# The order of the second batch's query tiles in two causal attention layers, and the store of the last rows

## The chip, the cores and the metric

The kernel is one program on 1 core of a Trainium2 chip. The metric is device time in microseconds (us) of one execution; three runs of the kernel before took 1541.68, 1546.62 and 1547.99, median 1546.62. The core's engines are TensorE (PE), VectorE (DVE), ScalarE (ACT), GpSimd (POOL) and SyncE (SP, which here issues DMAs); each works through its own instructions in order and waits on semaphores for the others.

## The reference

The input is x, two batches of 2048 tokens with 256 features, float32. Two layers are computed, each as x = x + attention(xn) + ffn(xn) with xn = layernorm(x):

```python
attn = einsum('bqd,bkd->bqk', q, k); attn = where(causal, -inf, attn) / sqrt(256)
attention = einsum('bqk,bkd->bqd', softmax(attn), v)
```

The feed-forward part of layer 0 is two shared experts and a routing of each token to 2 of 8 experts. That of layer 1 picks 255 of 2048 tokens of each batch by a router weight, sends them through a small transformer block, and leaves the other tokens as they are. Attention is causal over the 2048 tokens of a batch, so query tile i (128 rows) needs the keys of tiles 0 to i only: (i + 1) x 128 columns of scores.

## The kernel before, in words

The rows of x stay on chip in eight blocks of 512 rows (`x_blocks`, names x0 to x7; four blocks are a batch). A query tile is 128 rows; a batch has 16 of them, tiles 0 to 15, and tile i belongs to block i // 4 of its batch.

The program runs through: attention of layer 0 (line 348 gives its tile order), the routed experts (`run`, lines 671 on), the shared experts, in whose gaps the token selection of batch 0 is worked, and attention of layer 1, in whose gaps the selection of batch 1 is worked (`side`, `beside`, `step`). Both layers call the same function `attention` with the same list `in_turn`: the 16 tiles of the first batch upwards, and then the 16 tiles of the second batch downwards.

For each tile `attention` does this:

1. `scores` (L251 to L272). For each chunk of up to 512 keys PE makes a 128 x 512 score tile, in banks ps_sc and ps_tr by turns. DVE adds the causal mask on the last 128 columns (`tri`, L260), and copies the chunk into `row` with its maximum (L262). After the last chunk DVE reduces the maxima (L268), and ACT takes the exponential of the whole row at once (L270), up to 128 x 2048.
2. `turn` (L301, L303). POOL splits the float32 row into two planes of 16-bit halves for each chunk, and SP issues a DMA that transposes the planes (`across`).
3. `join` (L281, L282). DVE and ACT each copy one half of the transposed words back into a float32 tile, pT (six buffers). A join is put into the queues of DVE and ACT five pieces of work (`LAG`) after its chunk was turned, or when the values need it, whichever is earlier.
4. `average` (L316, L326). PE multiplies pT with the values, one product for each 128 keys, in bank ps_pv, and DVE scales the result and adds it to the row block.

Step 4 of a tile is issued behind step 1 of a later tile. The rule is in these lines, in which `p[2]` is the list of a waiting tile's chunks:

```python
for tile, later in zip(tiles, tiles[1:] + [None]):
    pending.append(turn(*scores(*tile)))
    if later:
        meet(later)
    while sum(len(p[2]) for p in pending[:-1]) >= 3:
        average(*pending.pop(0))
```

So a tile is averaged as soon as the waiting tiles other than the newest hold three chunks or more. `meet` projects the queries of a block of four tiles when the first tile of the block comes up (L594 in layer 0, L1387 in layer 1); the projected queries have two buffers.

The order in which the instructions stand in each engine's queue is made at build time by a scheduler, which may put an instruction that is ready early ahead of one that was written earlier.

Beside the attention of layer 0 the token rows are scattered to their experts' places by 64 indirect DMAs on POOL (L580), and the first expert weights (L684, 512 KB each) are loaded by SP ahead of the experts (L705). Beside the attention of layer 1 the selection (L1171, L1183, L1192, L1209 for its heads, L1002, L1263, L1275 for its norm and its feed-forward part, L1252 for its residual) ends with a scatter of the chosen rows (L1284); then `write_back` loads the gains by SP, 256 KB a piece, and DVE adds them to x (L1297). At the end a loop stores the eight blocks in order, 512 KB each (L1407); the scheduler puts each store into SP's queue near where its block becomes final.

Of the kernel before, what the change touches and what calls it, by code (L numbers as in the profile page):

```python
# [17 lines left out]
P = 128  # L18
B, S, D = 2, 2048, 256
NB = 8  # L20
BPB = NB // B
# [25 lines left out]
def transformer_kernel(ctx: ExitStack, tc: tile.TileContext, a: dict, out: bass.AP):  # L47
    nc = tc.nc
# [17 lines left out]
    x_blocks = []  # L66
# [8 lines left out]
    for g in range(NB):  # L75
# [8 lines left out]
        out=tri, in_=tri, compare_op=ALU.is_ge, fill=NEG, base=0, pattern=[[-1, P]], channel_multiplier=1  # L84
# [5 lines left out]
        out=before, in_=before, compare_op=ALU.is_gt, fill=0.0, base=0, pattern=[[1, P]], channel_multiplier=-1  # L90
# [27 lines left out]
    def step():  # L118
        while side:
            traced = nc.cur_bb.bb.instructions  # L120
            n = len(traced)
            got = next(side[0], step)
            for i in nc.cur_bb.bb.instructions[n:]:
                behind(i)
            held[0] = got == HOLD
            if got is not step:
                return
            side.pop(0)
# [216 lines left out]
            average(*late)  # L345


    in_turn = [(0, i) for i in range(S // P)] + [(1, i) for i in reversed(range(S // P))]

# [8 lines left out]
    with ExitStack() as l0:  # L360
# [8 lines left out]
        for dst, name in ((wq, "wq0"), (wk, "wk0")):  # L369
            turned = weight(work, name, "qT")  # L370
            ps = bank("mm")
            for ec in range(2):
                for dc in range(2):
                    k = (2 * ec + dc) * P
# [10 lines left out]
        parts = work.tile([P, 4, D], F32, tag="xn", name="parts", bufs=1)  # L385
# [286 lines left out]
    with ExitStack() as moe:  # L672
# [57 lines left out]
        for t in range(LIKELY):  # L730
            product, activated = run(t)
            if t >= LIKELY // 3:
                for dst, src in (next(coming, (None, None)),):
                    if dst is not None:
                        i = nc.scalar.dma_start(dst, src)
# [17 lines left out]
    for j, v in enumerate(_FREQ):  # L753
# [5 lines left out]
        out=head_of, in_=head_of, compare_op=ALU.is_ge, fill=0.0, base=0, pattern=[[-HD, 8]], channel_multiplier=1  # L759
    )  # L760
    nc.gpsimd.affine_select(
        out=head_of, in_=head_of, compare_op=ALU.is_ge, fill=0.0, base=HD - 1, pattern=[[HD, 8]],
# [640 lines left out]
    attention(att, in_turn, project_q1, values1, before_tile1)  # L1403
    while side:
        step()
    for g in range(NB):
        nc.sync.dma_start(  # L1407
            out[g * 512 : (g + 1) * 512, :].rearrange("(j p) d -> p j d", p=P), x_blocks[g]
        )


_PI = 3.1415925
# [58 lines left out]
```

## Time and profile before

| | |
|---|---|
| median of three runs | 1546.62 us |
| profiled execution | 1543.37 us, of which span 1541.7 us |
| mean granted PE clock | 0.993 |
| PE idle within the span | 63.5 us (1541.7 less 1478.2) |
| layer 0, batch 1: first scores | 213.11 us |
| routed experts: first matmul | 360.08 us |
| layer 1, batch 1: first scores | 1322.20 us |
| last value product ends, last store issued | 1536.92 us, 1537.47 us |

The times of places are counted from the start of the span. A line of PE's timeline gives start, duration, line, the tiles written and read, the shape, the number of records (a float32 matmul leaves two), and in brackets the time that PE was idle just before and what ended it. A line of the waits reads: who waited for whom, us in total, times, longest us. A row of the windows gives, for a stretch, busy time and count of PE, weight loads, DVE, ACT and POOL, then the granted PE clock (1.00 is full), the DMA engines' mean busy share, and GB/s.

### The profile page before, as it was taken

The numbers are of one execution on the slowest core, as the hardware profiler recorded it, in microseconds if no ns is written. First come the engines' busy times: TensorE is split into PE (matmuls) and PEld (weight loads), VectorE is DVE, ScalarE is ACT, GpSimd is POOL, SyncE is SP. The second block draws the span as 40 slices with busy tenths as digits, with TensorE's granted clock in tenths as the row PEclk, the third lists the DMA queues.
The fourth block names the chain that finished last, engine by engine and source line by source line (L and its number), as shares of the span: only waits on it lengthen the run. The fifth ranks groups of instructions, "written<-read, shape, count | busy, mean of one in ns | idle before, by whom it ended". The sixth has DMA issues, their size and how long they took to land.

```text
span 1541.7 us, 17887 instructions
## 1 busy us (share of the span) xinstructions
PE 1478.2 (96%) x5828; PEld 1050.5 (68%) x5828; DVE 697.3 (45%) x2055; ACT 442.0 (29%) x831; POOL 410.2 (27%) x596
## 2 busy tenths in 40 slices
PE   7999899998999999999999999999999998999998
PEld 4566566567888888888565565566675765577665
DVE  6346333343222222222244445866546468666354
ACT  2443233242111111111112212114633532344233
POOL 3554577532111111110122210231003213421132
PEclk9899999999999999999999999999999999999999
DMA  4844556666879888965001110040004425621144
GB/s 152 255 109 120 135 139 138 149 138 150 209 215 226 239 234 256 261 189 158 28 28 41 42 34 21 28 150 18 11 11 92 115 67 106 165 57 23 29 119 102
DMA packets 290558, 183.49 MB, mean 119 GB/s; under 512 B 192960, under 2 KB 265408, under 8 KB 290464
## 3 DMA queue, kind: packets, MB, share of 16 engines
q1 hardware_dynamic: 255168, 134.95, 36.0%
q10 hardware_dynamic: 27664, 26.53, 5.6%
q0 software_dynamic: 7632, 20.86, 4.4%
q8 instruction: 47, 0.77, 0.2%
q14 instruction: 47, 0.39, 0.1%
HBM read 93.14 MB, written 45.14 MB: 90 GB/s over the span
## 4 chain that ended last, share of the span: by engine, by line
PE 28%; issue 10%; DVE 7%; POOL 3%; DMA 2%; ACT 2%; SPq 0%; POOLq 0%; ACTq 0%; DVEq 0%
PE ps_tr L1338 6%; PE ps_sc L1338 6%; PE ps_pv L1357 5%; POOL planes L301 3%; DMA across<-planes 2%; PE ps_mm L1209 1%; PE ps_mm L1171 1%; DVE x L1368 1%; PE ps_sc L251 1%; PE ps_mm L801 1%; PE ps_mm L1192 1%; PE ps_pv L316 1%; PE ps_mm L1275 1%; DVE row L262 1%; ACT pr L1183 1%
## 5 line engine op out<-in xcount | busy, mean ns | idle before, releaser
L301 POOL COPY planes<-row 128x512 uint16<-128x512 uint16 (+3 forms) x320 | 167.7, 569 | 306.8 <-ACT row L270 293.8
L282 ACT COPY pT<-across 128x512 uint16<-128x512 uint16 (+3 forms) x160 | 106.3, 677 | 226.9 <-DMA across<-planes 211.7
L251 PE MATMUL ps_sc<-xnT,qT 128*128 128x512 f32 (+3 forms) x384 | 161.2, 541 | 0.3 <-DVE qT L150 0.2
L714 DVE SCALAR_TENSOR_TENSOR hid<-ps_tr,be,act 128x256 f32<-128x256 f32 x144 | 63.0, 479 | 197.9 <-PE ps_tr L705 192.9
L713 ACT ACTIVATE act<-ps_sc,be 128x256 f32<-128x256 f32 x144 | 60.4, 470 | 302.1 <-PE ps_sc L705 302.1
L1327 POOL DMA_INDIRECT ya<-sorted_y,place x64 | 62.2, 973 | 318.0 <-DVE x L1368 224.9
L316 PE MATMUL ps_pv<-vg,pT 128*128 128x256 f32 x544 | 129.0, 390 | 12.4 <-ACT pT L282 12.0
L705 PE MATMUL ps_sc<-xT,rw 128*128 128x256 f32 x576 | 136.2, 379 | 1.6 <-POOL xT L698 1.6
L705 PE MATMUL ps_tr<-xT,rw 128*128 128x256 f32 x576 | 136.1, 379 | 0.0
L316 PE MATMUL ps_pv<-v,pT 128*128 128x256 f32 x544 | 128.4, 381 | 7.0 <-ACT pT L282 4.6
L720 PE MATMUL ps_pv<-rw,hid 128*128 128x256 f32 x576 | 132.0, 382 | 0.0
L698 POOL COPY xT<-xs 128x512 uint16<-128x512 uint16 x72 | 51.3, 758 | 299.8 <-issue 281.9
L316 PEld LDWEIGHTS ps_pv<-vg,pT 128*128 128x128 f32 x544 | 104.6, 195 | 37.6 <-ACT pT L282 17.5
L1338 PE MATMUL ps_sc<-xnT,sw 128*128 128x512 f32 x256 | 121.9, 594 | 0.1
L1338 PE MATMUL ps_tr<-xnT,sw 128*128 128x512 f32 x256 | 122.0, 593 | 0.0
L316 PEld LDWEIGHTS ps_pv<-v,pT 128*128 128x128 f32 x544 | 101.3, 190 | 29.1 <-ACT pT L282 7.9
L705 PEld LDWEIGHTS ps_sc<-xT,rw 128*128 128x128 f32 x576 | 109.4, 190 | 16.8 <-POOL xT L698 2.0
L705 PEld LDWEIGHTS ps_tr<-xT,rw 128*128 128x128 f32 x576 | 109.5, 190 | 14.8
L720 PEld LDWEIGHTS ps_pv<-rw,hid 128*128 128x128 f32 x576 | 105.0, 190 | 21.2 <-DVE hid L714 6.7
L1357 PE MATMUL ps_pv<-sw,hid 128*128 128x256 f32 x512 | 117.5, 380 | 0.0
L1357 PEld LDWEIGHTS ps_pv<-sw,hid 128*128 128x128 f32 x512 | 96.6, 190 | 18.7 <-issue 6.2
L281 DVE COPY pT<-across 128x512 uint16<-128x512 uint16 (+3 forms) x160 | 68.8, 436 | 89.2 <-DMA across<-planes 88.3
(319 smaller groups left out, 1936.7 us busy)
## 6 DMA issues: line engine op xcount, KB each, us to landing
rw<-in_rw SPq DMA_DIRECT2D x108, 512.0 KB, 4.6
sorted_x<-zero ACTq DMA_DIRECT2D x13, 768.0 KB, 6.6
sorted_y<-y SPq DMA_DIRECT2D x36, 256.0 KB, 4.8
be<-biases SPq DMA_DIRECT2D x36, 132.0 KB, 4.5
table<-xn SPq DMA_DIRECT2D x8, 514.0 KB, 3.7
x<-in_x SPq DMA_DIRECT2D x8, 512.0 KB, 6.8
gains<-zero ACTq DMA_DIRECT2D x8, 512.0 KB, 3.2
gain<-gains SPq DMA_DIRECT2D x16, 256.0 KB, 2.7
```

The source lines that it names most:

```text
L251: product = nc.tensor.matmul(ps[:, :w], lhsT=qT[:, dc, (i % 4) * P : (i % 4 + 1) * P], rhs=xnT[g0 + k][:, dc, :w], start=(dc == 0), stop=( ...
L281: nc.vector.tensor_copy(words[:, :, 1], flat[:, :w]),
L282: nc.scalar.copy(words[:, :, 0], flat[:, w : 2 * w]),
L301: nc.gpsimd.tensor_copy(planes[:, h * w : (h + 1) * w], halves[:, :, 1 - h])
L316: product = nc.tensor.matmul(pv[:, :D], lhsT=turned[k][:, j : j + P], rhs=values[g0 + k][:, j // P, :D], start=(c + j == 0), stop=(c + j = ...
L705: nc.tensor.matmul(ps[:, k * TT : (k + 1) * TT], lhsT=we_in[:, dc, (h + k) * P : (h + k + 1) * P], rhs=xT[:, dc, :], start=(dc == 0), stop ...
L713: activated = nc.scalar.activation(act, p1[:, at], AF.Silu, bias=b1[:, hc])
L714: nc.vector.scalar_tensor_tensor(hid[:, h + k, :], p2[:, at], b2[:, hc], act, op0=ALU.add, op1=ALU.mult)
L720: product = nc.tensor.matmul(po[:, r, :], lhsT=hid[:, hc, r * P : (r + 1) * P], rhs=w3[:, hc, :], start=(hc == 0), stop=(hc == 3),)
L1327: nc.gpsimd.indirect_dma_start(out=ya, out_offset=None, in_=sorted_y, in_offset=bass.IndirectOffsetOnAxis(ap=place[rank][:, t : t + 1], ax ...
L1338: product = nc.tensor.matmul(ps, lhsT=ww[:, dc, hc * P : (hc + 1) * P], rhs=xnT[g][:, dc, :], start=(dc == 0), stop=(dc == 1),)
L1357: product = nc.tensor.matmul(po[:, :D], lhsT=hid[:, hc, j * P : (j + 1) * P], rhs=w["sw3", n][:, hc, :], start=(hc == 0), stop=(hc == 3),)
```

## The change

The first batch's tiles keep their order, in both layers. The second batch's tiles run as 15, 0, 14, 1, 13, 2, 12, 3, and then 4 to 11. At the end the block that holds the last tile is stored last, in two parts: its first three tiles of rows, and the last tile of rows (128 rows, 128 KB) by itself.

```diff
-    in_turn = [(0, i) for i in range(S // P)] + [(1, i) for i in reversed(range(S // P))]
+    in_turn = [(0, i) for i in range(S // P)]
+    in_turn += [(1, i) for k in range(4) for i in (15 - k, k)] + [(1, i) for i in range(4, 12)]
...
-    for g in range(NB):
-        nc.sync.dma_start(
-            out[g * 512 : (g + 1) * 512, :].rearrange("(j p) d -> p j d", p=P), x_blocks[g]
-        )
+    b, i = in_turn[-1]
+    last = b * BPB + i // 4
+    for g in [g for g in range(NB) if g != last] + [last]:
+        parts = (0, 3, 4) if g == last else (0, 4)
+        for lo, hi in zip(parts, parts[1:]):
+            nc.sync.dma_start(
+                out[g * 512 + lo * P : g * 512 + hi * P, :].rearrange("(j p) d -> p j d", p=P),
+                x_blocks[g][:, lo:hi, :],
+            )
```

## The prediction

> **What bounds the kernel now.** I read the engines' busy times first, then the waits of TensorE (PE), then PE's timeline in the two stretches the edit reorders, then one tile's way through all engines. Page part 1:
>
> ```profile
> PE 1478.2 (96%) x5828; PEld 1050.5 (68%) x5828; DVE 697.3 (45%) x2055; ACT 442.0 (29%) x831; POOL 410.2 (27%) x596
> ```
>
> PE is busy for 1478.2 of 1541.7 us, and the edit does not change the set of matmuls. A gain can only come from the 63.5 us in which PE idles, a loss only from new idling. Of the waits of PE the first entry is
>
> ```profile
> PE ps_pv L316 <- ACT pT L282: 16.6, 11, 3.7
> ```
>
> a value product that waits for its transposed probabilities. PE's timeline shows where this happens in the second batch of layer 0 (start, duration, records; in brackets the idle time before and its releaser):
>
> ```profile
> 284.89 5.45 PE L316 MATMUL ps_pv<-vg,pT 128*128 128x256 f32 x24 [1.44 <-ACT pT L282]
> ...
> 295.91 5.02 PE L316 MATMUL ps_pv<-vg,pT 128*128 128x256 f32 x22 [0.42 <-ACT pT L282]
> ...
> 309.75 6.27 PE L316 MATMUL ps_pv<-vg,pT 128*128 128x256 f32 x20 [2.37 <-ACT pT L282]
> ```
> ```profile
> 350.91 2.00 PE L316 MATMUL ps_pv<-vg,pT 128*128 128x256 f32 x8 [0.41 <-DVE x L326]
> 353.75 1.56 PE L316 MATMUL ps_pv<-vg,pT 128*128 128x256 f32 x6 [0.84 <-ACT pT L282]
> 356.68 1.80 PE L316 MATMUL ps_pv<-vg,pT 128*128 128x256 f32 x6 [1.37 <-ACT pT L282]
> 360.08 1.99 PE L705 MATMUL ps_sc<-xT,rw 128*128 128x256 f32 x8 [1.59 <-POOL xT L698]
> ```
>
> Together 8.44 us, of which 4.21 in the drain into the experts. The 20 records at 309.75 also took 6.27 us where 20 x 0.216 = 4.3 is usual (8 take 1.73): 1.95 lost to the clock. So this stretch wastes 10.4 us. In layer 1 the same kind of wait is 2.10 (at 1482.29) and 0.37, 0.77, 1.39 in the drain: 4.63. In all 15 us is what better cover could win; other waits there belong to the token selection beside it.
>
> How long is a tile's way from scores to values? Tile 14 of batch 1 in layer 0:
>
> ```profile
> 232.04 1.45 PE L251 MATMUL ps_tr<-xnT,qT 128*128 128x384 f32 x4
> ...
> 235.80 1.88 ACT L270 ACTIVATE row<-row,nmx 128x1920 f32<-128x1920 f32 x1
> ...
> 238.89 4.28 POOL L301 COPY planes<-row 128x512 uint16<-128x512 uint16 x8
> ...
> 243.51 0.77 ACT L282 COPY pT<-across 128x512 uint16<-128x512 uint16 x1 [5.74 <-DMA across<-planes]
> ```
>
> Scores end at 233.33; the first pT is there at 244.28, 10.95 us later; its four chunks follow 1.4, 1.5 and 0.8 us apart, faster than PE eats them (1.73 per chunk). PE had 12.9 us of other work between (value products 6.9, the next scores 6.0), so nothing waited.
>
> **The change, part by part.** Costs used: a 512-column score chunk 1.72 us (128: 0.43), a value product 0.432 per 128 keys, a query projection 3.44.
>
> *The reorder, layer 0.* No instruction is added but one store. What moves is the cover. `average` runs once the waiting tiles ahead of the newest hold three chunks. In the old order that puts a large tile between a tile's scores and its values. Now the next tile is a one-chunk tile, and with it the large tile's average falls due. The instruction order of the changed program shows what lies on PE between scores 14 and values 14: scores 1 (0.86), values 0 (0.43), scores 13 (6.02, pulled ahead), a quarter projection (0.86): 8.2 us. Against 10.95 that is a stall of 2.8. Bounds: 0.8, if POOL's scatters ahead of the planes (L580, about 2 us of the 10.95) were all done, to 2.8; eight scatters still stand there, so I take 2.8.
>
> Behind it a queue forms. On ACT, exp 13 stands behind tile 14's joins and behind tile 1's, and on DVE the last score pass of 13 stands behind the same joins. Counting from the end of scores 14: joins of 14 done 14.6; planes of 1 follow those of 14 and one scatter, transposed at 15.0, joined 15.5; then mask, pass and maximum on DVE to 16.4, exp 13 to 18.6 (1.8+0.2), scatters 1.1 as seen for tile 14, first planes 1.1, transpose 3.4, join 0.8: 25.0. PE by then has done values 14 (10.95 to 17.4), scores 2, values 1 and half a chunk of 12: 20.4. Stall 4.6 (3.5 without scatters, 4.9 if all three wait). Scores 12 follow values 13, and values 12 have scores 3, three quarters of a projection, values 2 and scores 4 as cover, 7.8 us and 0.2 of waiting for the query copy; exp 12 is on time, so the way is 8.5 to 9.6 (exp 1.68): stall 1.2, with that wait (0.8 to 1.9). Tiles 0 to 7 have covers of 9 us and more against about 8. The three expert weight loads (1.5 MB on SP), which caused the 2.37, now stand ahead of tile 6's transposes, where the cover is 14 us: I take 1.0 (0 to 2.4).
>
> *The drain, both layers.* Tile 11 is last, and between its scores and values stands only values 10: 11 x 0.432 = 4.75. Its way in a quiet kernel follows from tile 3 in layer 1:
>
> ```profile
> 1519.83 1.88 PE L251 MATMUL ps_sc<-xnT,qT 128*128 128x512 f32 x4
> ...
> 1523.39 0.72 ACT L270 ACTIVATE row<-row,nmx 128x512 f32<-128x512 f32 x1 [5.76 <-DVE nmx L268]
> ...
> 1529.43 2.00 PE L316 MATMUL ps_pv<-v,pT 128*128 128x256 f32 x8 [0.37 <-ACT pT L282]
> ```
>
> Scores end at 1521.54, values at 1529.43: 7.9; an exp over 1536 is 1.57 and not 0.72: 8.75. Stall 4.0 in each layer, where the small tiles lost 4.21 and 2.53. Chunks two and three come within 1.73 of each other and add nothing.
>
> *The clock.* Here rule and rows part. The Trainium skill ("TensorE: Matmul & The Clock Gate", Part 1) says that PE falls to half clock after an idle window of some 3.4 us and needs about as long of work to recover: 1.7 us lost for a gap over 3.4, nothing under. The rows of the stretches:
>
> ```profile
> 160.00:180.00 20.00, 15.99 (x49) 11.06 (x50) 6.72 (x21) 5.47 (x7) 8.81 (x14) 0.83 0.55 125
> ...
> 300.00:320.00 20.00, 17.64 (x53) 10.55 (x52) 5.65 (x18) 4.99 (x8) 4.30 (x10) 0.91 0.84 175
> ...
> 1300.00:1320.00 20.00, 16.47 (x80) 9.51 (x79) 16.56 (x37) 5.49 (x7) 9.08 (x15) 1.00 0.77 176
> ```
>
> The column after POOL is the granted clock. After a wait of 3.69 at 162.16, 24 records took 8.11 for 5.2 (2.9 lost); after 2.37, 1.95 lost; after 3.53 at 1305.96, nothing. So the length alone does not decide, and short gaps can cost; mean 1.6. By the rule the gaps 4.6, 4.0 and 4.0 cost 1.7 each, 5.1; by the rows 2.8, 4.6, 4.0, 4.0 cost 1.6 each, 6.4. I take the rows.
>
> Layer 0: 2.8 + 4.6 + 1.2 + 1.0 + 4.0 + 3 x 1.6 = 18.4, less 10.4: **+8.0**.
>
> *Layer 1.* The token selection's matmuls lie between the tiles. Before values 14 PE has 8.2 us, the way without scatters is 9.3 (DVE 1.9, exp 2.1, planes 1.1, transpose 3.4, join 0.8): 1.1. Scores 13 come late here, so its values have 11 us of cover and wait for nothing. Values 12: cover 7.4 and some 0.5 of selection waits, way 9.5 (the joins stand on DVE behind the residual adds L1252): 1.6. The next selection step, L1002, loses the 5.2 us of scores that covered its norm and gets values 12: 0.9. The gain adds L1297, each held by a load, stand on DVE ahead of the passes of tiles 4 to 6 as they did of 10 and 9: 1.5 for 2.10. Drain 4.0 + 1.6. Sum 10.7 less 4.63: +6.1. While PE waits for values the selection chain goes on, so some of its waits (7.4 us from 1338 to 1431) vanish: -1.0 (0 to -3).
>
> *The stores.* Four blocks of 512 KB used to end up late; now block x4 leaves in the middle, x7 and x5 under later tiles, all beside matmuls. SP issues them in order, so x4's store, which waits for tile 3's add, holds back the next gain load and the transposes of tile 5; 13 us of cover there, and 0.6 us an issue, so nothing, up to 1 if that cover fails. At the very end 128 KB lands instead of 512: 3.2 us for 512 and 2.7 for 256 (the gain loads) give about 2.45: -0.75.
>
> Layer 1 with the stores: **+4.3**. Sum +12.3. The profiled execution took 1543.37 (span 1541.7 and 1.7 around it): 1555.7. The median, 1546.62, is 3.25 above that run: I forecast **1558.9** as median.
>
> **The rivals.** *Uncovered large tiles*, as summed: chance 0.5, 1553 to 1565. *It spreads further*: every clock loss is the 2.9 seen once (4 x 1.3 more), the scatters hold tile 13 fully and the weight loads bite as before (+1.7), so +19.2, 1565.8; for it speaks that joins, passes and exps share strict queues; against it, that the small tiles of layer 0 have ample cover: 0.17. *It cancels*: the clock mostly stays up, as after the 3.53, and the selection absorbs layer 1's waits: 12.3 - 6.4 - 2 = +3.9, 1550.5: 0.25. *The small tiles really fill*: the place is values 14, 13 and 12 of both layers. If a large tile's first pT comes within the 8.2 us of cover, these waits and the queue behind exp 13 are gone, and with the weight loads and gain adds hidden too only the two drains of 4.0 stay of the 15.0 us: 8.0 - 15.0 - 0.75 = -7.75, 1538.9. It decides at 8.2, and the trace has 10.95, which only an empty POOL brings near: 0.08. That the drain with small tiles was the larger waste is true only for layer 0 (4.21 for 4.0).
>
> **How the numbers follow.** Something like 0.5% (7.7 us) is what a measurement of this kernel tells from no change. The likeliest case lies over it mostly, the second wholly, the third under it: slower 0.66, within 0.26, faster 0.08. The range reaches over these three and, with the bounds of the unknown terms, some 10 us to either side of the sum; it leaves out the gain and the case of every bound at one end: 1549 to 1570.
>
> **What would show it.** In the changed profile: a bracket of 2 to 3 us before values 14 and of 4 to 5 before values 13 in layer 0 (about 253 and 267 us), 4 us before the last 24 records of both layers, granted clock under 1.00 beside them, "PE ps_pv L316 <- ACT pT L282" up from 16.6 to about 30, and the last store under 4 us before the end. I am wrong if PE runs from scores 14 to values 12 without brackets, if the clock stays 1.00, or if the loss sits in the selection's lines (L1192, L1002).

## The result and the profile after

The changed kernel takes 1552.95 us (median of 18 runs, 1547.87 to 1557.53) and the kernel before, on the same chip, 1545.08 (18 runs, 1541.68 to 1549.73). The ratio is 1.0048, 95% interval 1.0036 to 1.0060, so the change costs about 7.4 us. The forecast was 1558.9 with a range of 1549 to 1570: the sign and the range held, the size (+12.3) was too large.

Some short names are used from here on. "Scores 14" and "values 14" are the score matmuls and the value products of tile 14 of the second batch. Its cover is what PE has to do between the two. Its way is the time from the end of its scores to its first transposed probabilities (pT). PE waits when the way is longer than the cover.

The profiled execution of after is one of its slower ones: 1557.31 us, span 1555.6, mean granted clock 0.987. First its page, part 1, and the two first entries that concern value products in the waits of PE:

```profile
PE 1486.3 (96%) x5828; PEld 1053.9 (68%) x5828; DVE 699.6 (45%) x2055; ACT 441.9 (28%) x831; POOL 410.5 (26%) x596
```
```profile
PE ps_pv L316 <- ACT pT L282: 18.5, 13, 3.5
...
PE ps_pv L316 <- DVE pT L281: 5.4, 2, 3.7
```

The same 5828 matmuls keep PE busy for 8.1 us longer. PE waits only 5.8 us more (69.3 for 63.5). Of the 8.1, 6.4 lie in the two stretches that the edit reorders (4.6 in layer 0, 1.8 in layer 1), and these grew by 10.4 us together. So more than half of the profiled difference is matmuls that ran slower, and a table of waits alone would miss it. PE's timeline of layer 0's second batch shows both (start, duration; in brackets the idle time before):

```profile
259.57 9.53 PE L316 MATMUL ps_pv<-vg,pT 128*128 128x256 f32 x30 [3.71 <-DVE pT L281]
272.74 5.45 PE L316 MATMUL ps_pv<-vg,pT 128*128 128x256 f32 x24 [0.63 <-DVE x L326]
278.34 1.13 PE L316 MATMUL ps_pv<-vg,pT 128*128 128x256 f32 x4 [0.15 <-ACT pT L282]
293.80 6.05 PE L316 MATMUL ps_pv<-vg,pT 128*128 128x256 f32 x26 [1.84 <-ACT pT L282]
...
361.73 8.37 PE L316 MATMUL ps_pv<-vg,pT 128*128 128x256 f32 x24 [3.33 <-ACT pT L282]
371.78 1.99 PE L707 MATMUL ps_sc<-xT,rw 128*128 128x256 f32 x8 [1.68 <-POOL xT L700]
```

These are values 14, values 13 (two rows), values 12, values 11 and the first expert. Thirty records of value products take 6.64 us where nothing disturbs them, and 9.53 behind the wait of 3.71; 24 records take 5.45, and 8.37 behind the wait of 3.33. The granted clock, the column of the windows after POOL's, shows the same places, with a full clock between them:

```profile
260.00:280.00 20.00, 19.22 (x70) 14.72 (x70) 6.96 (x24) 7.63 (x12) 11.94 (x18) 0.87 0.71 141
280.00:300.00 20.00, 18.16 (x64) 11.31 (x63) 9.36 (x32) 8.26 (x14) 14.20 (x20) 1.00 0.55 125
...
360.00:380.00 20.00, 16.59 (x62) 13.62 (x63) 3.60 (x8) 5.25 (x8) 5.29 (x10) 0.83 0.37 67
```

In layer 1 the rows that matter are values 12, the selection's L1004, values behind the gain adds, and the drain on tile 11:

```profile
1453.98 3.70 PE L316 MATMUL ps_pv<-v,pT 128*128 128x256 f32 x16 [1.67 <-DVE pT L281]
1459.24 0.81 PE L1004 MATMUL ps_mm<-ident,hn 128*128 128x128 f32 x4 [1.56 <-DVE hn L1024]
1491.52 2.00 PE L316 MATMUL ps_pv<-v,pT 128*128 128x256 f32 x8 [1.60 <-ACT pT L282]
...
1544.95 7.14 PE L316 MATMUL ps_pv<-v,pT 128*128 128x256 f32 x24 [3.33 <-ACT pT L282]
```

Two stretches sum this up. Layer 0's runs from the first scores of the second batch's tile 15 to the experts' first matmul; layer 1's from its first scores of that tile to the end of the span. Layer 0's was 360.08 - 213.11 = 146.97 us and is 371.78 - 216.30 = 155.48: +8.51. Layer 1's was 219.50 and is 1555.6 - 1334.24 = 221.36: +1.86, the stores included. The spans differ by 13.9. Of this, 3.19 lie ahead of the first changed instruction (213.11 and 216.30); in the nine other kernels below that leave everything ahead of it unchanged, it began at anything from 208.75 to 215.45, so that part is spread between executions. So a profile of one execution is read by stretches here and not by its span.

### The profile page after: what moved, and what is told of

It is laid out like the page before. It is cut to its first block, busy times and chain, and to the rows that moved or that the text cites. A ratio compares the mean times of both kernels' runs of the same rounds, so it can differ in the third digit from the quotient of the medians.

```text
span 1555.6 us, 17898 instructions
## 1 busy us (share of the span) xinstructions
PE 1486.3 (96%) x5828; PEld 1053.9 (68%) x5828; DVE 699.6 (45%) x2055; ACT 441.9 (28%) x831; POOL 410.5 (26%) x596
## 4 chain that ended last, share of the span: by engine, by line
PE 28%; issue 10%; DVE 6%; DMA 3%; POOL 3%; ACT 1%; SPq 0%; POOLq 0%; ACTq 0%; DVEq 0%
PE ps_tr L1340 6%; PE ps_sc L1340 6%; PE ps_pv L1359 5%; POOL planes L301 3%; DMA across<-planes 2%; PE ps_pv L316 2%; PE ps_mm L1173 1%; DVE x L1370 1%; PE ps_mm L1211 1%; PE ps_sc L251 1%; PE ps_mm L1265 1%; PE ps_mm L803 1%; PE ps_mm L1194 1%; PE ps_tr L251 1%; PE ps_mm L1277 1%
## 5 line engine op out<-in xcount | busy, mean ns | idle before, releaser
L282 ACT COPY pT<-across 128x512 uint16<-128x512 uint16 (+3 forms) x160 | 105.7, 677 | 219.3 <-DMA across<-planes 203.8
L316 PE MATMUL ps_pv<-vg,pT 128*128 128x256 f32 x544 | 134.8, 401 | 15.8 <-ACT pT L282 11.5
L316 PE MATMUL ps_pv<-v,pT 128*128 128x256 f32 x544 | 130.9, 385 | 10.6 <-ACT pT L282 7.0
L316 PEld LDWEIGHTS ps_pv<-vg,pT 128*128 128x128 f32 x544 | 107.6, 201 | 43.2 <-ACT pT L282 22.1
L316 PEld LDWEIGHTS ps_pv<-v,pT 128*128 128x128 f32 x544 | 102.1, 192 | 35.3 <-ACT pT L282 14.9
```

What stands on the lines that cost most here:

```text
L282: nc.scalar.copy(words[:, :, 0], flat[:, w : 2 * w]),
L316: product = nc.tensor.matmul(pv[:, :D], lhsT=turned[k][:, j : j + P], rhs=values[g0 + k][:, j // P, :D], start=(c + j == 0), stop=(c + j = ...
```

## The experiments

Every kernel below was timed beside the kernel before on the same chip, in rounds on several chips, so ratios are compared rather than medians (the median of before was 1544.5 to 1545.2). Stretches are of the one profiled execution; without the change they were 146.97 and 219.50. They contain whatever the clock did in that execution.

| kernel | median us | ratio to before, 95% | layer 0 | layer 1 |
|---|---|---|---|---|
| after | 1552.95 | 1.0048 [1.0036, 1.0060] | 155.48 | 221.36 |
| layer0_alone | 1554.65 | 1.0061 [1.0037, 1.0086] | 153.80 | 219.60 |
| layer1_alone | 1545.85 | 1.0008 [0.9996, 1.0019] | 145.32 | 219.30 |
| end_at_11 | 1552.60 | 1.0052 [1.0037, 1.0067] | 153.54 | 222.46 |
| pairs_alone | 1548.28 | 1.0027 [1.0016, 1.0038] | 150.58 | 219.04 |
| longer_cover | 1549.69 | 1.0031 [1.0019, 1.0042] | 153.53 | 215.66 |
| longer_cover_pairs | 1548.67 | 1.0026 [1.0013, 1.0039] | 156.54 | 216.44 |
| filled_end | 1550.17 | 1.0035 [1.0024, 1.0047] | 152.73 | 218.74 |
| store_alone | 1543.99 | 1.0000 [0.9988, 1.0012] | 146.90 | 223.52 |
| no_scatters_before | 1538.88 | 0.9960 [0.9944, 0.9975] | 140.27 | 221.08 |
| no_scatters_after | 1547.67 | 1.0022 [1.0010, 1.0034] | 150.44 | 219.71 |
| no_scatters_covered | 1534.64 | 0.9928 [0.9909, 0.9947] | 142.84 | 217.82 |
| layer1_covered | 1540.09 | 0.9961 [0.9946, 0.9975] | 143.87 | 216.61 |

### One layer at a time

```diff
+    in_turn1 = [(0, i) for i in range(S // P)] + [(1, i) for i in reversed(range(S // P))]
...
-    attention(att, in_turn, project_q1, values1, before_tile1)
+    attention(att, in_turn1, project_q1, values1, before_tile1)
```

(layer0_alone, with the old stores; layer1_alone has the two lists exchanged and the split store.)

> New order in layer 0 only; layer 1's order and the stores are those of before. Before is 1545.1 us, after 1553.0. Theory A (large tiles whose values come due behind a one-chunk tile, tile 11's uncovered drain, and half clock behind both gaps; these are worst in layer 0, where exp carries no selection work but the queues of ACT and DVE do): the profile of after lost 8.5 us in this stretch, some 3 of it clock that varies between runs, so +5 to +8, 1550 to 1553; waits of about 3.7 us before values 14 and 3.3 before values 11. Rival B (the loss is shared evenly by the two layers): +3 to +4, 1548.5. Rival C (the loss is the store or lies in layer 1): 0, 1545.

> New order in layer 1 only, with the split store; layer 0 as before. Theory A: the profile of after lost 1.9 us in this stretch with the store's 1.3 taken off already, so 0 to +2, 1545 to 1547; waits of about 3.3 before values 11 and under 2 before values 14, 13 and 12. Rival B (even shares): +3 to +4 less nothing, 1548.5. Rival C (layer 1 carries the loss): +7, 1552. In its profile scores 15 of the second batch in layer 0 should begin at 213 us as before, not at 216, if the three microseconds ahead of the edit were caused by the edit; if they begin anywhere from 213 to 217, that is a spread of runs.

Layer 0 alone costs 9.4 us (1.0061, 5.7 to 13.3 by the interval), a little over the +5 to +8 of theory A, with waits of 3.70 before values 14 and 3.40 before values 11. Layer 1 alone costs 1.2, and the interval includes zero. Theory A has the place right in both; even shares (B) and layer 1 as the seat (C) fall. The scores of tile 15 began at 208.75 in layer1_alone, outside the 213 to 217 that I had named, and with layer 0 untouched: the three microseconds ahead of the edit are not the edit's.

### The ending and the pairs

```diff
-    in_turn += [(1, i) for k in range(4) for i in (15 - k, k)] + [(1, i) for i in range(4, 12)]
+    in_turn += [(1, i) for i in (15, 14, 13, 12)] + [(1, i) for i in range(12)]
```

(end_at_11; pairs_alone keeps the pairs and ends with `reversed(range(4, 12))`.)

> Second batch's tiles 15, 14, 13, 12, then 0 to 11 in both layers, with the split store: no alternation, but the same three-chunk tile last. Theory A (alternation and ending each cost): the waits before values 14 and 13 go (cover is a four-chunk tile), at most 1 us is left before values 12, and the drain keeps its 3.3 us and its clock loss of 2 to 3 in each layer. That is about 10 in layer 0 against 10.4 before, and about +2 less the store's 1.3 in layer 1: 0 to +2, 1545 to 1547. Rival D (the ending is the whole loss): +7, 1552.

> Second batch's tiles 15, 0, 14, 1, 13, 2, 12, 3, then 11 down to 4 in both layers, with the split store: the alternation, with a two-chunk tile last. Theory A: layer 0 keeps about 6 us of waits before values 14, 13 and 12 and 3 of clock, and its drain falls to values of a two-chunk tile behind another (cover 1.3 to 2.2 against a way of some 6.5: 4 to 5 of wait): the ending is no better than tile 11's, so +4 to +8, 1549 to 1553. Rival D (the ending on tile 11 is the whole loss): 0 or under, 1543 to 1545. Theory A would also hold if the last wait is shorter than tile 11's and the sum +2 to +4.

The time of end_at_11, +8, is what rival D said, but the profile does not support D. The drain is the same 3.33, and here its 24 records took an undisturbed 5.45 in layer 0. What my expectation missed is the step from tile 12 down to tile 0:

```profile
271.34 3.78 PE L316 MATMUL ps_pv<-vg,pT 128*128 128x256 f32 x8 [4.94 <-DVE x L326]
...
314.06 2.97 PE L251 MATMUL ps_sc<-xnT,qT 128*128 128x512 f32 x4 [2.89 <-ACT qT L600]
357.51 5.45 PE L316 MATMUL ps_pv<-vg,pT 128*128 128x256 f32 x24 [3.33 <-ACT pT L282]
```

Values 12 wait 4.94 where I allowed 1: a single small tile behind a large one is enough, and the copy of projected queries (2.89) was late as well. So this run does not isolate the ending. pairs_alone does better, for its layer 0 keeps the wait of 3.72 before values 14 and has 1.83 in place of 3.33 before its last values. At +4.2 us it lies at the lower edge of what theory A gave and outside D's "0 or under". So the pairs cost even with a short ending; that the ending on tile 11 costs as well rests on its drain in the profiles and on the 3 us between the ratios of pairs_alone and after, whose intervals just touch.

### More cover for the large tiles

```diff
-            while sum(len(p[2]) for p in pending[:-1]) >= 3:
+            while sum(len(p[2]) for p in (pending[1:] if pending[0][0] else pending[:-1])) >= 3:
```

> The order of after, but in the second batch the values of a tile are multiplied only once three chunks of later tiles have their scores, counted behind that tile and not with it; so the values of 15, 14, 13 and 12 come behind the next four-chunk tile's scores. Theory A (cover decides): cover before values 14 rises from 8.2 us to some 14 (values 15, values 0, scores 1, scores 13) against a way of about 11.9 seen, so the waits before values 14, 13 and 12 (6.3 us in after) go, and the clock loss behind the first of them (3.1, 1.9 and 2.8 in three profiles) with it; the drain on tile 11 stays. 1553.0 - 6 - 2.5 = about 1544, no more than 1547. Rival E (it is the queues of ACT and DVE, which carry the same number of joins either way, that are late, not the cover): the waits move and stay near 6 us: 1551 to 1555.

> As the run with the longer cover, but with 11 down to 4 at the end in place of 4 to 11. Theory A: both costs are gone (pairs alone had a drain wait of 1.8 before its last values and 1.6 for the experts' rows); layer 0's stretch keeps about 4 us of waits against 8.4 and 2 of clock before, and layer 1 the store's 1 to 1.3: 1545.1 - 6 - 1 = about 1538 (1535 to 1541), faster than before. Rival E: near pairs alone, 1546 to 1549.

Theory A failed here in layer 0, where the stretch stayed at 153.5. The waits before values 14 to 12 did go, but others came before scores, 7.5 us in the four rows below. They moved and stayed, as rival E said, though the time (1549.69) lies between the two forecasts:

```profile
252.46 1.99 PE L251 MATMUL ps_sc<-xnT,qT 128*128 128x512 f32 x4 [1.85 <-DVE row L262]
269.80 3.09 PE L251 MATMUL ps_sc<-xnT,qT 128*128 128x512 f32 x4 [2.42 <-DVE row L262]
288.41 2.33 PE L251 MATMUL ps_sc<-xnT,qT 128*128 128x512 f32 x4 [1.58 <-ACT qT L600]
316.90 1.98 PE L251 MATMUL ps_sc<-xnT,qT 128*128 128x512 f32 x4 [1.61 <-ACT qT L600]
```

Scores wait for DVE to empty their banks. What held DVE before 269.80 is seen by following tile 13 back, through DVE, POOL and ACT:

```profile
267.96 0.46 DVE L281 COPY pT<-across 128x512 uint16<-128x512 uint16 x1 [5.65 <-DMA across<-planes]
```
```profile
258.71 0.96 POOL L582 DMA_INDIRECT sorted_x<-rows,place  x1 [0.30 <-issue]
...
262.51 0.96 POOL L582 DMA_INDIRECT sorted_x<-rows,place  x1 [0.30 <-issue]
263.47 4.06 POOL L301 COPY planes<-row 128x512 uint16<-128x512 uint16 x8
```
```profile
258.15 1.79 ACT L270 ACTIVATE row<-row,nmx 128x1792 f32<-128x1792 f32 x1 [2.92 <-DVE nmx L268]
```

The exp of tile 13 ends at 259.94. POOL works through scatters until 263.47 before it touches the planes, 3.5 us later. DVE's join, waiting for the transposed planes, stands in front of DVE's next mask and passes, so the late planes stop the scores of the next tile. This gave a new theory, that the scatters are the cause, and three runs to test it (below). In layer 1, where no such scatters run, the longer cover worked: 215.66 and 216.44, less than the old order's 219.50.

longer_cover_pairs missed its 1538 by 10 us and came out where rival E put it. Its layer 0 took 156.54, with the same waits before scores (1.89 and 2.44) and one of 4.69 before values 10 that has another cause: the transposes for these values were issued at 312.95, right behind loads of expert weights, and the first took 6.9 us to land, where those of the tile before took 3.3 and 4.7.

### Filling the last pause

```diff
+            if (b, i) == in_turn[-1]:
+                fill = bank("mm")
+                for _ in range(4):
+                    nc.tensor.matmul(fill, lhsT=ident, rhs=xnT[g0][:, 0, :], start=True, stop=True)
             pv = bank("pv")
```

> The order of after, with four matmuls of 128x512 (0.86 us each) whose result nobody reads set before the values of tile 11 at the end of each layer, so that TensorE idles under 0.5 us there in place of 3.3; nothing that the values need comes earlier. Theory A with the clock as a cost of the idle time itself: the 24 products then take 5.2 to 5.5 us in both layers; in six drains on tile 11 seen so far they took 8.4, 7.1, 7.1, 7.1, 5.5 and 5.5, so 1.6 each on the mean comes back: 1553.0 - 3.2 = 1550, less up to 0.4 for the filler's own end. Rival F (the lower clock comes from what ran in the microseconds before, not from the pause): no gain, 1553 to 1554, and the products still at 7 to 8 in some drain.

The median is the 1550 forecast, though the intervals of this kernel and of after overlap. The profile decides:

```profile
355.77 5.45 PE L320 MATMUL ps_pv<-vg,pT 128*128 128x256 f32 x24 [0.48 <-ACT pT L282]
...
1536.61 5.46 PE L320 MATMUL ps_pv<-v,pT 128*128 128x256 f32 x24 [0.47 <-ACT pT L282]
```

With PE kept occupied the 24 products take 5.45 and 5.46 (and 5.46 in layer1_covered, filled the same way). Behind the same pause left empty, of 3.33 to 3.40 us, twelve drains of these runs took once 8.37, six times 7.01 to 7.14, once 6.95, and four times 5.45 or 5.46; the mean is 6.65. So the idle pause costs 1.2 us of clock on average on top of itself, and it costs nothing one time in three. Three filled drains without loss are few beside that; they speak against rival F and do not exclude it.

### The store by itself

```diff
-    for g in range(NB):
-        nc.sync.dma_start(
-            out[g * 512 : (g + 1) * 512, :].rearrange("(j p) d -> p j d", p=P), x_blocks[g]
-        )
+    for g in [g for g in range(NB) if g != last] + [last]:
+        j = i % 4
+        parts = ((0, j), (j + 1, 4), (j, j + 1)) if g == last else ((0, 4),)
...
```

> The order of before, with the last tile's rows stored by themselves (128 KB, the other three tiles of that block ahead of it). All theories: the tail from the end of the last values to the end of the span falls from 4.8 to about 3.5 us, so -0.8 to -1.3: 1544. A rival that only the tile-11 ending lets the other rows leave early (before ends with tiles 3, 2, 1, 0, whose rows are all late): 0 to -0.4.

The tail from the last value product to the end of the span is 4.10 us for 4.78 before and 3.51 in after: 0.7 and 1.3 gained. The times do not resolve that: 1.0000, interval 0.9988 to 1.0012. The profiled execution shows how much larger the spread is. In layer 1 the same matmuls kept PE busy for 206.4 us, for 202.0 before, at a granted clock of 0.97 for 1.00. Some of this lies behind a pause of 0.68 us, where the 8 records of the second row take 1.99 in the profile of before.

```profile
1426.43 1.15 PE L1192 MATMUL ps_mm<-ident,pr 128*128 128x128 f32 x4 [1.83 <-ACT pr L1183]
1428.26 3.78 PE L1209 MATMUL ps_mm<-wide,apart 128*128 128x256 f32 x8 [0.68 <-ACT wide L152]
```

### Without the scatters

```diff
             for t in range(n):
                 for rank in range(2):
-                    i = nc.gpsimd.indirect_dma_start(
-                        out=sorted_x,
-                        out_offset=bass.IndirectOffsetOnAxis(ap=place[rank][:, t : t + 1], axis=0),
-                        in_=rows[t // 4][:, t % 4, :], in_offset=None,
-                    )
...
                     yield
```

> The order of before with the same 64 scatters left out. Theory G: in the old order the large tiles have 12 us and more of cover, so the scatters hide nearly everywhere; at most the wait of 1.4 us before one four-chunk tile's values goes, and the 2.4 behind the expert weights stays: 0 to -2, 1543 to 1545. Then the two orders differ without scatters by 2 to 4 us (the drain on tile 11 and its clock), in place of 7. Theory A without G: the orders still differ by 6 or more, this one at 1543 to 1545 and the order of after at 1551.

> The order of after, with the 64 indirect DMAs that scatter the rows by expert left out (L582: GpSimd is busy 0.96 us in each, 1.27 from one to the next; the experts then compute on zeros, the instructions of every other engine are the same). To be read against the order of before with the same left out. Theory G (the lost time of layer 0 is GpSimd's: three or more scatters stand between a large tile's exp and its planes, so its way is longer than any cover that the order gives; that is also why a longer cover only moved the waits): the waits before values 14, 13 and 12 fall from 3.7, 0.6 and 1.9 us to under 1 in all, and the half clock behind the first goes; layer 0's stretch falls from 155.5 to 147 to 150 and the time by 6 to 8 against after, to 1545 to 1547. Theory A without G (cover alone, the scatters being 1.1 to 2 us of the way): before values 14 a wait of 2.0 to 2.7 stays, and the time falls by 2 or so, 1551.

> The order of after with the longer cover and with the 64 scatters left out (so the experts compute on zeros). Asked: why the longer cover moved layer 0's waits in place of removing them. Theory H (the scatters: four to seven of them, 1.27 us each, stood between a large tile's exp and its planes there, and the joins, waiting for these, held DVE and with it the score passes of the next large tile): without them the waits of 1.9 and 2.4 before scores vanish, layer 0's stretch falls from 153.6 us to 144 or 145 (140.3 in the old order without scatters, and 3 to 5 for the drain on tile 11 and its clock), and the time to 1537 to 1540, at most 2 above the old order without scatters. Theory I (the fixed order of joins and passes on ACT and DVE does it, scatters or not): waits of 4 us and more stay before the scores or the values of 14 to 12, the stretch at 148 or more, the time 1543 or more.

Theory G, that the scatters alone make the new order slow, falls: without them the orders differ by 8.8 us (1547.67 and 1538.88), no less than with them. Each theory had a part right. The new order came near the 1545 to 1547 of G, and the old one gained 6.1 us, where neither theory had given it more than 2. The wait before values 14 did fall to 1.08, but another took over:

```profile
252.00 6.72 PE L316 MATMUL ps_pv<-vg,pT 128*128 128x256 f32 x30 [1.08 <-DVE pT L281]
264.10 8.00 PE L316 MATMUL ps_pv<-vg,pT 128*128 128x256 f32 x28 [2.36 <-DVE x L326]
285.42 5.88 PE L316 MATMUL ps_pv<-vg,pT 128*128 128x256 f32 x26 [1.28 <-ACT pT L282]
...
353.12 7.01 PE L316 MATMUL ps_pv<-vg,pT 128*128 128x256 f32 x24 [3.36 <-ACT pT L282]
361.81 1.99 PE L700 MATMUL ps_sc<-xT,rw 128*128 128x256 f32 x8 [1.68 <-POOL xT L693]
```

Cover and scatters together settle it (theory H). From the first scores to the experts, no_scatters_covered has only the two last rows of that list left, and one of 0.27:

```profile
339.12 1.56 PE L316 MATMUL ps_pv<-vg,pT 128*128 128x256 f32 x6 [0.27 <-ACT pT L282]
344.04 7.13 PE L316 MATMUL ps_pv<-vg,pT 128*128 128x256 f32 x24 [3.35 <-ACT pT L282]
```

Layer 0's stretch is 155.5 in the new order, 153.5 with the longer cover, 150.4 without the scatters and 142.8 with both. Each alone gives 2 to 5 us and the two 12.6. Part of this is the clock, but the waits alone (the stretch less PE's busy time in it, 143.1, 140.5, 140.1 and 137.5) say the same: 12.4, 13.1, 10.3 and 5.3 us. A large tile is late when its cover is shorter than its way. The longer rule adds cover, but while scatters stand ahead of the planes the joins come late, and these hold up the score passes on DVE and with them the cover itself. All waits that are left are the drain's.

Leaving the scatters out takes away POOL's time and also what the scatters move (125 GB/s fall to 96 in the stretch of the new order). The runs do not part the two; the rows of POOL above, where the planes stand behind the scatters for 3.5 us, speak for its queue.

### A version faster than both

Layer 0 in the old order; layer 1 in the new one with the longer cover, the split store and the fill ahead of tile 11's values.

```diff
...
-            while sum(len(p[2]) for p in pending[:-1]) >= 3:
+            while sum(len(p[2]) for p in (pending[1:] if shifts is None and pending[0][0] else pending[:-1])) >= 3:
...
```

> Meant to beat both: layer 0 in the order of before; layer 1 in the new order with the longer cover (the values of a tile only when three chunks stand behind it), the split store, and the four unread matmuls ahead of tile 11's values at the end of layer 1 only. Layer 1's stretch was 219.5 us before, 221.4 after, 219.3 with its new order alone, and 215.7 with the longer cover, where no scatters run beside it. If that last is the cover: 1544.5 - 3.5 - up to 1 for the clock of the drain = 1540 to 1541.5, faster than before. If it was one lucky execution with a high clock (1.00 against 0.99 to 1.00 in the others): 1544 to 1546.

1540.09 us, ratio 0.9961 (0.9946 to 0.9975): by the medians 4.9 us faster than before, by the ratio 6.0. This is as forecast. Layer 1's stretch is 216.6, and its drain reads

```profile
1530.11 5.46 PE L320 MATMUL ps_pv<-v,pT 128*128 128x256 f32 x24 [0.47 <-ACT pT L282]
```

The new order and the split store alone cost 1.2 us (layer1_alone), so the gain comes with the longer cover and the fill. The old order under the longer rule was not run: whether the new order has a part in the gain stays open.

## Why the prediction was right, and where its size was not

**Layer 0, the sum.** Forecast 18.4 us of waste less 10.4, +8.0. Measured in the profile +8.51; layer0_alone, timed, +9.4 (interval 5.7 to 13.3). The place and the mechanism were right: cover against way. Its terms were less so; that the sums agree is luck, for their errors cancelled:

| term | forecast us | profile of after |
|---|---|---|
| wait before values 14 | 2.8 | 3.71 |
| before values 13 | 4.6 | 0.63 + 0.15 |
| before values 12 | 1.2 | 1.84 |
| weight loads, other waits | 1.0 | 0.78 + 0.25 |
| drain | 4.0 | 3.33 + 1.68 |
| clock | 4.8 | 6.2 |
| sum | 18.4 | 18.6 |

(The clock's 6.2 is PE's busy time in the stretch, 143.13, less the 136.91 that the same 490 records take in layer1_covered, whose clock there is 1.00; the two rows, of PE alone, are below, after first. The wait of 0.78 is before scores 8.)

```profile
216.30:371.80 155.50, 143.13 (x490) 0.96 0.58 125
214.97:358.90 143.93, 136.91 (x490) 1.00 0.60 136
```

**Values 14.** The cover of 8.2 us was exact (scores end at 247.69, the projection's quarter at 255.86). The way was 11.9 and not 10.95: the last of the scatters ahead of the planes ends 2.7 us after the exp, where 1.1 had been counted, and DVE's pass of tile 13 stood ahead of its join. That pass itself waited 6.30 us for POOL's planes, which the forecast had not seen.

```profile
249.08 1.90 ACT L270 ACTIVATE row<-row,nmx 128x1920 f32<-128x1920 f32 x1 [7.67 <-DVE nmx L268]
...
252.77 0.96 POOL L582 DMA_INDIRECT sorted_x<-rows,place  x1 [0.30 <-issue]
253.74 4.28 POOL L301 COPY planes<-row 128x512 uint16<-128x512 uint16 x8
...
258.05 0.75 DVE L262 TENSOR_SCALAR_CACHE_REDUCE row<-ps_sc,shift 128x512 f32<-128x512 f32 x1 [6.30 <-POOL planes L301]
```

From the code I read this as the row's two buffers: tile 13 takes the one that tile 14 holds, with only tile 1 between, where in the old order it takes tile 15's. No run tried a third buffer.

**Values 13: the failed term.** The forecast's reckoning of the other engines was right: first pT of 13 at 25.0 us behind scores 14, and ACT had it at 272.69, 25.0 after 247.69. (DVE's add L326, which PE waited for last, ended at 272.74; it stood behind DVE's join of the same chunk.)

```profile
271.92 0.77 ACT L282 COPY pT<-across 128x512 uint16<-128x512 uint16 x1 [4.69 <-DMA across<-planes]
```

What failed is the sum "4.6 + 1.6": a wait that ends at a time set by other engines and a clock loss just ahead of it do not add. PE spent on values 14 what it would have waited before values 13. Duration of values 14 plus that wait is 9.53 + 0.63 in after, 8.40 + 1.83 in layer0_alone, 9.32 + 0.91 in pairs_alone and 9.48 + 0.58 in filled_end: 10.1 to 10.2 in all four, whatever the clock did. These two rows of layer0_alone, set against those of after, show the exchange:

```profile
258.71 8.40 PE L316 MATMUL ps_pv<-vg,pT 128*128 128x256 f32 x30 [3.70 <-DVE pT L281]
271.95 6.43 PE L316 MATMUL ps_pv<-vg,pT 128*128 128x256 f32 x28 [1.83 <-DVE x L326]
```

The forecast had 6.5 + 1.6 + 4.6 = 12.7 here: 2.5 too much.

**The drain.** The wait was 3.33 (forecast 4.0) in all twelve, within 0.07. The way was 8.9 for 8.75, but the cover, from 352.81 to 358.40 in layer 0 of after, was 5.6 for 4.75; a wait of 0.25 within values 10 is part of that. And the 4.21 that it was to replace in layer 0 held 1.59 of waiting for the experts' rows, and that wait stays, as 1.68. The forecast dropped it.

**The weight loads.** "Which caused the 2.37" fits the trace. In before the three loads were issued at 297.91, and the transposes for values 9 right behind them, at 299.78; the first of these took 9.1 us to land, where the three just before had taken 3.3 at the median. In no_scatters_before the loads were issued 6.7 us ahead of the same transposes, these took 3.3 at the median, and PE did not wait.

```profile
297.91 1.58 SPq L684 DMA_DIRECT2D rw<-in_rw  x3
299.78 9.38 SPq L303 DMA_TRANSPOSE across<-planes  x3
```
```profile
292.13 1.57 SPq L677 DMA_DIRECT2D rw<-in_rw  x3
...
298.79 13.84 SPq L303 DMA_TRANSPOSE across<-planes  x6
```

What the forecast had not seen is that the scatters have a part in it: without them the loads move away from the transposes, and the waits of 1.44 and 0.42 are gone too. Layer 0 is 6.7 us shorter. The old order paid for the scatters as well. No run held the loads back to test them by themselves.

**The clock.** The forecast began by saying that a loss can only come from new idling of PE; its own term for the clock says otherwise, and the profile does too. Where rule and rows parted, the rows were right that length does not decide: pauses of 3.33 to 3.40 us, at or just under the rule's 3.4, lost clock in eight drains of twelve. The size was near the 1.7 that the forecast estimated from the rule: seven of the eight lost 1.5 to 1.7, one 2.9. The profile of after lost more than the mean of 1.6 (2.9 us each behind values 14 and 11, 1.7 at the end); over twelve drains the mean is 1.2. That fits a median below what the profiled execution says. The losses of 2.9 and 1.95 that the forecast took from before are some 0.2 too large, because it counted 5.2 us for 24 records, and an undisturbed row of 24 reads 5.45. The Trainium skill ("TensorE: Matmul & The Clock Gate", Part 1, "What's actually happening") also says that the idle window runs freely, so that the same kernel meets it at another phase in each run; four drains of twelve without loss fit that, the pause of 0.68 with 1.8 us of loss does not follow from its 3.4.

**Layer 1.** Forecast +4.3 with the stores; the profile has +1.86, and layer1_alone +1.2 (-0.6 to +2.9) in time. Values 12 (1.6 forecast, 1.67) and the wait at the gain adds (1.5, 1.60) were close, values 14 (1.1, then 0.44 + 0.18) and L1004 (0.9, then 1.56) less so. The mis-sized term is the selection's own waits in the stretch where its heads are worked: 7.44 us before, 1.33 + 0.73 + 1.05 = 3.11 after, so -4.3 where I took -1.0. The longest of before, and then all of after:

```profile
1344.66 1.13 PE L1109 MATMUL ps_mm<-f_wq,hT 128*128 128x256 f32 x4 [1.75 <-ACT part L152]
1363.15 0.44 PE L1192 MATMUL ps_mm<-ident,pr 128*128 128x128 f32 x2 [1.11 <-ACT pr L1183]
1427.60 0.93 PE L1192 MATMUL ps_mm<-ident,pr 128*128 128x128 f32 x4 [1.84 <-ACT pr L1183]
```
```profile
1349.07 1.95 PE L1389 MATMUL ps_mm<-xnT,wqk 128*128 128x512 f32 x4 [1.33 <-DVE hT L1010]
1392.59 0.44 PE L1194 MATMUL ps_mm<-ident,pr 128*128 128x128 f32 x2 [0.73 <-ACT pr L1185]
1427.88 0.44 PE L1194 MATMUL ps_mm<-ident,pr 128*128 128x128 f32 x2 [1.05 <-ACT pr L1185]
```

The forecast's reason, that the selection's chain on DVE and ACT goes on while PE waits for values or works on them, fits this; no run took the selection away to show it.

**The stores.** -0.75 forecast; the tail of after is 1.27 shorter and that of store_alone 0.68. Right in sign, not resolved in time.

**The base.** The three runs of before that the forecast started from had a median of 1546.62; with 18 it is 1545.08. So 1.5 us of the miss of 5.9 is the base, and 4.4 the size. Some 2.4 of these are layer 1, by the profile; in layer 0's profile the terms cancel. The other 2 are not resolved: they lie between one profiled execution and the median of 18.

**The rivals.** "It cancels" (+3.9) is nearer to +7.4 than the forecast's +12.3, by 3.5 against 4.9, and has its two reasons in part: the clock stayed up in some drains, and the selection absorbed most of layer 1. "It spreads further" and "the small tiles really fill" did not occur. The latter's condition, a first pT within the cover, needed both an empty POOL and another rule.

**The signs.** A wait before values 14 (3.7 for 2 to 3), the waits in the drains, a clock under 1.00 beside them and the last store under 4 us before the end all came. The wait of 4 to 5 before values 13 did not, and "PE ps_pv L316 <- ACT pT L282" rose to 18.5 and not to about 30: 5.4 stand under DVE's pT, and the wait before values 13 went into the slower values 14.

## What to carry to other kernels

When an order is changed under a rule that counts what is pending, work out for each item what lies on the bottleneck engine between its producer and its consumer, and compare it with the way through every other queue, side work in those queues included: here cover and scatters each gave 2 to 5 us alone and 12.6 together. A wait whose end is set by other engines absorbs a slowdown of the waiting engine just ahead of it, so do not add the two. And where a stage has side work that waits already, look whether a new wait on the bottleneck takes over time that was idle before.

## What the runs showed of the hardware

What a pause costs in clock differed from execution to execution: behind pauses of 3.33 to 3.40 us eight of twelve drains lost 1.5 to 2.9 us, four nothing. A pause of 0.67 or 0.68 in layer 1 (L1209 of before), with one of 1.83 or 1.84 shortly ahead of it, was followed by 1.99, 1.99, 3.39, 3.51 and 3.78 us for the same eight records in five profiles. Four unread matmuls in the pause brought three drains of three to 5.45 or 5.46.

An indirect DMA of this kernel occupies POOL for 0.96 us, and in a row of them the next starts 1.27 us after it. By that, 64 hold POOL for some 81 us (an estimate), and leaving them out took 6.1 us off the old order, although POOL is busy for only 27% of the span. A transpose issued by SP right behind three loads of 512 KB took 9.1 us to land, for a median of 3.3 in the three just before.
